# Layer norms of a graph network: mean and deviation applied by ScalarE instead of VectorE, biases and own features added by VectorE instead of TensorE

## The chip, the cores and the metric

The kernel runs on one core of a Trainium2 chip. The metric is the device time of one execution in microseconds (us). A core has five engines that run their own instruction streams and wait for each other by semaphores: TensorE (PE in the profile; PEld is its weight loading), VectorE (DVE), ScalarE (ACT), GpSimd (POOL) and SyncE (SP), which here issues transfers. Matmul results land in PSUM, everything else lives in SBUF with 128 partitions. A tile "128x512" has 512 elements in each of 128 partitions.

## The reference, cut to what matters

There are 16 graphs ("entries") of 1024 nodes with 64 features, each with a 1024 x 1024 weighted adjacency. Four layers follow each other; each adds its result to its input and applies a layer norm without learned scale:

```python
def _layernorm(x, axis=-1, eps=1e-5):
    m = jnp.mean(x, axis=axis, keepdims=True)
    v = jnp.var(x, axis=axis, keepdims=True)
    return (x - m) / jnp.sqrt(v + eps)

# layer 0: messages, then a two-layer MLP on [x, messages]
dh = jnp.tanh(jnp.concatenate([x, adj @ x], -1) @ W1 + b1) @ W2 + b2
x = _layernorm(x + dh)
# layer 1: mean over neighbours
x = _layernorm(x + (adj / jnp.clip(jnp.sum(adj, 2, keepdims=True), 1.0, None)) @ x)
# layers 2 and 3: thin out the neighbours, take per feature a weighted sum of the
# 0.25, 0.5 and 0.75 quantiles over each node's neighbours (agg), then an MLP
y = (relu((x + agg) @ W1 + b1) @ W2 + b2) * mask[..., None]
x = _layernorm(x + y)
```

So one entry has four layer norms, 64 in all.

## The kernel before

Nodes stand on partitions: one entry's features are a tile of 128 x (8 x 64), "NT = 8" tiles of 64 features, C = 64, processed in two halves of G = 4 tiles. For the quantiles, each node's neighbours are gathered by POOL from a table in memory into a ring (`got_s`), or, for the nodes with most neighbours, picked by matmuls with one-hot matrices (`hot`, `pgk`); VectorE sorts the gathered lists with min and max networks (`got_s`, `other`, `got`), and ScalarE multiplies the sorted rows by weights.

The order of the program is made by hand: the sorting of round k is the main thread, and the other parts (features and lists of later entries, the end of earlier ones) are Python generators. A counter adds up VectorE's estimated time, and `yield 7` means: the next piece of this generator is emitted once VectorE has been given about 7 us more of work. Each engine executes its own instructions in the emitted order.

The layer norm:

```python
def settle(dst, y, chain):
    st = s.work.tile([P, 4, NT], F32, name=f"ln_st_{chain}", bufs=1)
    dve.reduce_sum(st[:, 0], y, axis=AX.X)
    dve.tensor_scalar(st[:, 1], st[:, 0], 1.0 / C, None, op0=ALU.mult)
    dve.tensor_sub(y, y, st[:, 1, :, None].to_broadcast([P, NT, C]))
    yield 2
    nc.scalar.activation(dst, y, AF.Square)
    yield 7
    dve.reduce_sum(st[:, 2], dst, axis=AX.X)
    yield 1
    nc.scalar.activation(st[:, 3], st[:, 2], AF.Sqrt, bias=eps, scale=1.0 / C)
    yield 6
    dve.reciprocal(st[:, 0], st[:, 3])
    dve.tensor_mul(dst, y, st[:, 0, :, None].to_broadcast([P, NT, C]))
```

The first two layers, with cuts:

```python
def features(b, e):
    # ... x_s and the adjacency tiles adj[i] are loaded
    for h in range(NH):                     # two halves of 512 nodes
        # ... px: transposed x_s (L417) and messages (L421), node_in
        nc.tensor.matmul(px[:C], w01s, node_in, start=True, stop=True)
        yield 9
        nc.scalar.activation(hid_t, px[:C], AF.Tanh, bias=b01c)
        yield 3
        pd = s.psum.tile([P, G, C], F32, name="pd", tag="x", bufs=1)
        for q in range(G):
            nc.tensor.matmul(pd[:, q, :], hid_t[:, q * P : (q + 1) * P], w02s, start=True, stop=False)
            nc.tensor.matmul(pd[:, q, :], ones_row, bias_rows[0], start=False, stop=False)     # L438
            nc.tensor.matmul(pd[:, q, :], ident, x_s[:, h * G + q, :], start=False, stop=True) # L439
        yield 10
        nc.scalar.copy(y[:, h * G : (h + 1) * G], pd)                                          # L441
    yield 4
    yield from settle(x1[:, :, :C], y, "x")
    # ...
    for h in range(NH):
        # ... pa = adjacency times x1, with the row sum in column C (L454); near from adj
        dve.tensor_scalar(deg[:, 0], pa[:, :, C], 1.0, None, op0=ALU.max)
        dve.reciprocal(deg[:, 1], deg[:, 0])
        yield 1
        for q in range(G):                                                                     # L465
            nc.scalar.activation(y[:, h * G + q, :], pa[:, q, :C], AF.Copy, scale=deg[:, 1, q : q + 1])
    yield 5
    dve.tensor_add(y, y, x1[:, :, :C])
    yield from settle(x2, y, "x")
    # ...
```

The end of layers 2 and 3 (`agg` holds the quantile sums, `xc` the layer's input):

```python
def finish(b, e, layer, agg):
    for h in range(NH):
        pt = s.psum.tile([P, HALF], F32, name="pt", tag="m", bufs=1)
        for q in range(G):
            # transpose and add in PSUM: xc (L763), agg (L764)
            nc.tensor.matmul(pt[:C, q * P : (q + 1) * P], xc[:, h * G + q, :], ident, start=True, stop=False)
            nc.tensor.matmul(pt[:C, q * P : (q + 1) * P], agg[:, h * G + q, :], ident, start=False, stop=True)
        # ... o_t = copy of pt; ph = w1s times o_t; h_t = relu(ph + b1c)
        pd = s.psum.tile([P, G, C], F32, name="pd", tag="m", bufs=1)
        for q in range(G):
            nc.tensor.matmul(pd[:, q, :], h_t[:, q * P : (q + 1) * P], w2s, start=True, stop=False)
            nc.tensor.matmul(pd[:, q, :], ones_row, bias_rows[1 + layer], start=False, stop=True)  # L778
        yield 9
        for t in range(h * G, (h + 1) * G):                                                        # L781
            nc.scalar.activation(y[:, t, :], pd[:, t - h * G, :], AF.Copy, scale=e.mask[:, t : t + 1])
    yield 4
    dve.tensor_add(y, y, xc)
    yield from settle(xn, y, "m")
    # ... xn is written to the table of the next layer, or to the output, by eight POOL transfers
```

The one-hot selections, the largest user of PE, are emitted from `pick` (L349) for one row of 24 matmuls at a time, after VectorE has made the one-hot matrix `hot`, of which four can exist at once.

Of the kernel before, what the change touches and what calls it, by code (L numbers as in the profile page):

```python
# [12 lines left out]
F32 = mybir.dt.float32  # L13
# [4 lines left out]
AF = mybir.ActivationFunctionType  # L18
ALU = mybir.AluOpType
AX = mybir.AxisListType  # L20

P = 128
# [5 lines left out]
KS = -(-(max(SIZES[:-1]) - 1) // 8) * 8  # L28
KW = max(SIZES)
HOTS = 4  # L30
ROOM = 75
LONG = 40
BIG = 1e30
EPS = 1e-5
# [178 lines left out]
def adj_resnorm_kernel(ctx: ExitStack, tc: tile.TileContext, x, adj_t, nodemask, w01, b01, w02, b02,  # L213
                       w21, b21, w22, b22, w31, b31, w32, b32, out):
    nc = tc.nc
    B, N, C = x.shape
    NT = N // P
# [3 lines left out]
    s = SimpleNamespace()  # L221
    dve = Metered(nc.vector)
# [47 lines left out]
    def row(ap, name):  # L270
        return weight(ap.rearrange("(o c) -> o c", o=1), name)

    def column(ap, name):
        return weight(ap.rearrange("(c o) -> c o", o=1), name)

    w01s, b01c, w02s = weight(w01, "w01s"), column(b01, "b01c"), weight(w02, "w02s")
    mlps = [
        (weight(w21, "w21s"), column(b21, "b21c"), weight(w22, "w22s")),
        (weight(w31, "w31s"), column(b31, "b31c"), weight(w32, "w32s")),
    ]  # L280
    bias_rows = [row(b, f"bias_row{i}") for i, b in enumerate((b02, b22, b32))]
    ones_row = const.tile([1, P], F32, name="ones_row")
    nc.vector.memset(ones_row, 1.0)
# [78 lines left out]
    def settle(dst, y, chain):  # L362

        st = s.work.tile([P, 4, NT], F32, name=f"ln_st_{chain}", bufs=1)
        dve.reduce_sum(st[:, 0], y, axis=AX.X)
        dve.tensor_scalar(st[:, 1], st[:, 0], 1.0 / C, None, op0=ALU.mult)
        dve.tensor_sub(y, y, st[:, 1, :, None].to_broadcast([P, NT, C]))
        yield 2
        nc.scalar.activation(dst, y, AF.Square)
        yield 7  # L370
        dve.reduce_sum(st[:, 2], dst, axis=AX.X)
        yield 1
        nc.scalar.activation(st[:, 3], st[:, 2], AF.Sqrt, bias=eps, scale=1.0 / C)
# [17 lines left out]
    G = HALF // P  # L391

    def features(b, e):
# [18 lines left out]
        for h in range(NH):  # L412

            node_in = s.work.tile([P, HALF], F32, name="node_in", bufs=1)
            px = s.psum.tile([P, HALF], F32, name="px", tag="x", bufs=1)
            for q in range(G):
                nc.tensor.transpose(px[:C, q * P : (q + 1) * P], x_s[:, h * G + q, :], ident)  # L417
# [14 lines left out]
            hid_t = s.work.tile([C, HALF], F32, name="hid_t", tag="node_in", bufs=1)  # L432
            nc.scalar.activation(hid_t, px[:C], AF.Tanh, bias=b01c)
            yield 3
            pd = s.psum.tile([P, G, C], F32, name="pd", tag="x", bufs=1)
            for q in range(G):
                nc.tensor.matmul(pd[:, q, :], hid_t[:, q * P : (q + 1) * P], w02s, start=True, stop=False)
                nc.tensor.matmul(pd[:, q, :], ones_row, bias_rows[0], start=False, stop=False)  # L438
                nc.tensor.matmul(pd[:, q, :], ident, x_s[:, h * G + q, :], start=False, stop=True)  # L439
            yield 10  # L440
            nc.scalar.copy(y[:, h * G : (h + 1) * G], pd)  # L441
# [5 lines left out]
        for h in range(NH):  # L447
            pa = s.psum.tile([P, G, C + 1], F32, name="pa", tag="x", bufs=1)
            for q in range(G):
                i = NT + h * G + q  # L450
                t = i - NT
# [303 lines left out]
    def finish(b, e, layer, agg):  # L755

        xc = e.xs[layer]
        w1s, b1c, w2s = mlps[layer]
        y = s.work.tile([P, NT, C], F32, name="y_m", bufs=1)
        for h in range(NH):  # L760
            pt = s.psum.tile([P, HALF], F32, name="pt", tag="m", bufs=1)
            for q in range(G):
                nc.tensor.matmul(pt[:C, q * P : (q + 1) * P], xc[:, h * G + q, :], ident, start=True, stop=False)  # L763
                nc.tensor.matmul(pt[:C, q * P : (q + 1) * P], agg[:, h * G + q, :], ident, start=False, stop=True)  # L764
# [9 lines left out]
            yield 3  # L774
            pd = s.psum.tile([P, G, C], F32, name="pd", tag="m", bufs=1)
            for q in range(G):
                nc.tensor.matmul(pd[:, q, :], h_t[:, q * P : (q + 1) * P], w2s, start=True, stop=False)
                nc.tensor.matmul(pd[:, q, :], ones_row, bias_rows[1 + layer], start=False, stop=True)  # L778
            yield 9
            for t in range(h * G, (h + 1) * G):  # L780
                nc.scalar.activation(y[:, t, :], pd[:, t - h * G, :], AF.Copy, scale=e.mask[:, t : t + 1])  # L781
# [178 lines left out]
    def per_row(ap):  # L960
        t = s.work.tile([P, C], F32, name="per_row")
        nc.sync.dma_start(t, ap.rearrange("(o c) -> o c", o=1).to_broadcast([P, C]))
        return t

    def transposed(src, name):

        dst = s.work.tile([C, N], F32, name=name, bufs=1)
# [7 lines left out]
    def layer0(adj_half, x_s, x1):  # L975
# [21 lines left out]
        nc.vector.tensor_add(y, y, per_row(b02)[:, None, :].to_broadcast([P, NT, C]))  # L997
        nc.vector.memset(x1[:, :, C : C + 1], 1.0)
        layernorm(x1[:, :, :C], y)

# [15 lines left out]
        nc.vector.tensor_add(y, y, x1[:, :, :C])  # L1016
        layernorm(x2, y)

    def mlp(xc, agg, mask, layer, dst):
        w1s, b1c, w2s = mlps[layer]  # L1020
# [12 lines left out]
        nc.vector.tensor_add(y, pd, per_row((b22, b32)[layer])[:, None, :].to_broadcast([P, NT, C]))  # L1033
# [131 lines left out]
    with tc.If(nc.values_load(over_d[:, B:]) > 0):  # L1165
        with tc.For_i(0, B) as b:
            with tc.If(nc.values_load(over_d[:, ds(b, 1)]) > 0), ExitStack() as general:
# [32 lines left out]
                for layer, (xc, xn) in enumerate(((x2, x3), (x3, x1[:, :, :C]))):  # L1200
                    with tc.tile_pool(name=f"g_lists{layer}", bufs=1) as lists:
                        long_quantiles(lists, table[layer][0], idx, wts, agg)
                    with tc.tile_pool(name=f"g_dense{layer}", bufs=1) as dense:
                        dense_quantiles(dense, xc, valid, count, longest, agg)
                    mlp(xc, agg, mask, layer, xn)
# [34 lines left out]
```

## Time and profile before

| | |
|---|---|
| time, median of 3 runs | 5350.52 us (5345.66 to 5353.45) |
| span of the profiled execution | 5351.7 us, 110787 instructions |
| granted TensorE clock, mean | 0.745 of full speed |
| busiest groups on VectorE | min and max of the sorts; `hot` 449.3 us; near, takes, order |
| POOL | 2944 gathers, mean 1134 ns; 256 row writes |

The profile is of one execution. "Busy" is the time in which an engine executes; an engine that waits for a semaphore is not busy. A group line names line, engine and operation, output and inputs, the number of instructions, then busy us and mean ns of one, then the idle time just before them and what ended it. Line numbers of VectorE are mostly L207, a helper through which all its instructions of the main program pass; so VectorE's work is told apart by the tiles that it reads and writes. A line of waits reads: who waited, on whom, us in total, how many times, longest us. The chain that ended last consists of POOL's last output writes alone, so it does not show what set the time; the stages and the waits have to do it.

### The profile page before, as it was taken

How to read it: one execution, taken by the hardware profiler on the slowest of the kernel's cores; microseconds unless marked ns; L12 is line 12 of the kernel's file. 1: busy time of each engine (PE TensorE's matmuls, PEld its weight loads, DVE VectorE, ACT ScalarE, POOL GpSimd, SP SyncE). 2: the span in 40 equal slices, each digit the busy share in tenths (PEclk: the TensorE clock that was granted, in tenths of full speed). 3: DMA queues.
4: the chain of work that ended last, by engine and by line, in shares of the span. 5: the costliest groups of instructions: out<-in, count | busy, mean ns of one | idle time of the engine just before them, and what ended most of it. 6: DMA issues, size and time to landing. Idle time of an engine off the chain costs nothing. (4 is left out here: it accounts for less than half of the span.)

```text
span 5351.7 us, 110787 instructions
## 1 busy us (share of the span) xinstructions
PE 3747.4 (70%) x44869; PEld 2907.4 (54%) x44936; DVE 4588.7 (86%) x9200; ACT 2052.9 (38%) x5056; POOL 3650.5 (68%) x3228
## 2 busy tenths in 40 slices
PE   7857476778785866858588795949588695726343
PEld 5746255656574655647376573737476574625332
DVE  2495667999999989798998989999988999998976
ACT  2352342435352624435252624444343535212211
POOL 0425626777777777767677777787777878787572
PEclk7877677788686877868687787879687786756555
DMA  2212212222222221222222131222222221111010
GB/s 82 77 31 50 45 40 59 52 60 57 58 54 58 46 55 41 59 54 57 56 56 58 39 74 36 55 49 58 58 56 59 54 48 21 27 21 26 16 24 10
DMA packets 420176, 259.27 MB, mean 48 GB/s; under 512 B 106164, under 2 KB 368452, under 8 KB 419652
## 3 DMA queue, kind: packets, MB, share of 16 engines
q0 software_dynamic: 102400, 105.06, 10.2%
q1 hardware_dynamic: 317252, 147.02, 9.7%
q8 instruction: 353, 5.78, 0.5%
q14 instruction: 171, 1.40, 0.1%
HBM read 239.27 MB, written 12.58 MB: 47 GB/s over the span
## 5 line engine op out<-in xcount | busy, mean ns | idle before, releaser
L353 POOL DMA_INDIRECT got_s<-table,idx x2944 | 3338.6, 1134 | 1461.1 <-issue 775.9
L349 PEld LDWEIGHTS <-hot 128*128 128x128 bf16 x24576 | 977.3, 109 | 763.3 <-DVE hot L207 656.2
L349 PE MATMUL pgk<-x2p,hot 128*128 128x64 bf16 x12288 | 538.7, 210 | 340.1 <-DVE hot L207 331.9
L349 PE MATMUL pgk<-x3p,hot 128*128 128x64 bf16 x12288 | 543.3, 210 | 262.8 <-DVE hot L207 237.1
L512 PE MATMUL pr<-steps,near 128*128 128x512 bf16 x1469 | 403.1, 430 | 257.0 <-ACT junk L518 154.1
L207 DVE TENSOR_TENSOR other<-got_s 128x512 f32<-128x512 f32 (+8 forms) x900 | 516.4, 583 | 57.5 <-issue 35.9
L743 ACT ACTIVATE got_s<-got_s,wts 128x64 f32<-128x64 f32 x1568 | 400.8, 337 | 343.3 <-DVE got_s L207 342.6
L207 DVE TENSOR_SCALAR hot<-place 128x1024 bf16<-128x1024 f16 x1024 | 449.3, 441 | 89.0 <-PE pgk L349 88.7
L207 DVE TENSOR_TENSOR got_s<-got_s 128x384 f32<-128x384 f32 (+7 forms) x918 | 492.0, 538 | 19.0
L598 PE MATMUL pk<-near,order 128*128 128x512 f16 x2048 | 487.9, 394 | 17.3 <-DVE order L207 13.9
L454 PE MATMUL pa<-x,adj_r 128*128 128x65 f32 x2048 | 398.6, 379 | 134.8 <-DMA adj_r<-in_adj_dram 49.8
L454 PEld LDWEIGHTS pa<-x,adj_r 128*128 128x128 f32 x2048 | 387.1, 293 | 140.9 <-DMA adj_r<-in_adj_dram 50.1
L512 PEld LDWEIGHTS <-near 128*128 128x128 f16 x1536 | 162.0, 108 | 475.2 <-issue 349.6
L207 DVE TENSOR_TENSOR got_s<-other 128x512 f32<-128x512 f32 (+8 forms) x774 | 408.6, 540 | 7.2
L555 PE MATMUL pv<-minus_n,takes 128*128 128x128 bf16 x1024 | 206.3, 237 | 197.2 <-DVE takes L207 195.0
L598 PEld LDWEIGHTS <-order 128*128 128x128 bf16 x2048 | 200.0, 101 | 260.8 <-issue 41.0
L207 DVE TENSOR_TENSOR other<-other 128x128 f32<-128x128 f32 (+13 forms) x558 | 319.0, 572 | 14.9
L518 ACT ACTIVATE junk<-pr,nb_st 128x1024 f16<-128x1024 f32 x256 | 281.8, 1107 | 43.9 <-PE pr L512 42.8
L207 DVE TENSOR_TENSOR other<-got 128x128 f32<-128x128 f32 (+5 forms) x270 | 232.7, 881 | 59.1 <-ACT got L733 56.4
L421 PE MATMUL px<-adj_r,x_s 128*64 128x128 f32 x2048 | 272.3, 291 | 4.0 <-ACT node_in L424 2.9
L743 ACT ACTIVATE got<-got,wts 128x64 f32<-128x64 f32 x672 | 165.0, 335 | 268.0 <-DVE got L207 268.0
L421 PEld LDWEIGHTS px<-adj_r,x_s 128*64 128x64 f32 x2048 | 243.6, 147 | 22.5 <-issue 12.8
(201 smaller groups left out, 6953.6 us busy)
## 6 DMA issues: line engine op xcount, KB each, us to landing
adj_r<-in_adj_dram SPq DMA_DIRECT2D x256, 512.0 KB
got_s<-table,idx POOLq DMA_INDIRECT x2944
x_s<-in_x_dram SPq DMA_DIRECT2D x16, 256.0 KB
table<-x SPq DMA_DIRECT2D x16, 256.0 KB
x<-table SPq DMA_DIRECT2D x16, 256.0 KB
table<-x3s,rows POOLq DMA_INDIRECT x128
out_dram<-agg,out_rows POOLq DMA_INDIRECT x128
table<-no_row SPq DMA_DIRECT2D x6, 0.2 KB
```

The costliest lines, as they stand in the source:

```text
L207: return call(*args, **kwargs)
L349: nc.tensor.matmul(dst, hot[:, c, :], parts[:, c, q, :], start=first and c + q == 0, stop=c == NT - 1 and q == 2)
L353: nc.gpsimd.indirect_dma_start(out=dst, out_offset=None, in_=tab, in_offset=bass.IndirectOffsetOnAxis(ap=rows, axis=0))
L421: nc.tensor.matmul(px[C:, q * P : (q + 1) * P], x_s[:, jt, :], adj[t][:, jt, :], start=jt == 0, stop=jt == NT - 1)
L454: nc.tensor.matmul(pa[:, q, :], adj[i][:, jt, :], x1[:, jt, :], start=jt == 0, stop=jt == NT - 1)
L512: nc.tensor.matmul(pr[:, h * HALF : (h + 1) * HALF], near[:, c, t * P : (t + 1) * P], steps[:, ONSET + h * HALF - c * P :][:, :HALF], star ...
L518: nc.scalar.activation(junk, prs[t - 1], AF.Sign, bias=lim[:, i, t - 1 : t], scale=-1.0, accum_out=cut_at[:, i, t - 1 : t])
L555: nc.tensor.matmul(pv[:, cols], takes[:, c, rows], minus_n, start=False, stop=False)
L598: nc.tensor.matmul(cols, order[:, c, t * P : (t + 1) * P], left(c, slice(h * G, (h + 1) * G)), start=c == 0, stop=c == NT - 1)
L743: nc.scalar.activation(prods[:, m, i, :], got[:, m, slot_id, :], AF.Copy, scale=e.wts[:, t, i : i + 1])
```

## The change

In the layer norms ScalarE subtracts the mean and multiplies by the reciprocal deviation, one tile of 64 features at a time, because its per-partition bias and scale hold one value for each partition. VectorE loses these two passes. In exchange, what PE and ScalarE did for VectorE elsewhere goes back to it: the biases, the own features and the sum of `xc` and `agg` are no longer added by matmuls in PSUM, and the degree and the mask are no longer multiplied in by ScalarE. It is another division of the same work among the engines. The biases are now kept as rows spread over all partitions, and the space of the old bias rows lets the gather ring have one row more.

```diff
-ROOM = 75
+ROOM = 76
...
-    w01s, b01c, w02s = weight(w01, "w01s"), column(b01, "b01c"), weight(w02, "w02s")
+    w01s, b01c, w02s, b02r = weight(w01, "w01s"), column(b01, "b01c"), weight(w02, "w02s"), per_row(b02, "b02r")
... (b22r and b32r likewise, in place of bias_rows and ones_row)
@@ settle
-        dve.tensor_scalar(st[:, 1], st[:, 0], 1.0 / C, None, op0=ALU.mult)
-        dve.tensor_sub(y, y, st[:, 1, :, None].to_broadcast([P, NT, C]))
+        dve.tensor_scalar(st[:, 1], st[:, 0], -1.0 / C, None, op0=ALU.mult)
         yield 2
+        for t in range(NT):
+            nc.scalar.activation(y[:, t, :], y[:, t, :], AF.Identity, bias=st[:, 1, t : t + 1])
         nc.scalar.activation(dst, y, AF.Square)
-        yield 7
+        yield 9
         dve.reduce_sum(st[:, 2], dst, axis=AX.X)
         yield 1
         nc.scalar.activation(st[:, 3], st[:, 2], AF.Sqrt, bias=eps, scale=1.0 / C)
         yield 6
         dve.reciprocal(st[:, 0], st[:, 3])
-        dve.tensor_mul(dst, y, st[:, 0, :, None].to_broadcast([P, NT, C]))
+        yield 1
+        for t in range(NT):
+            nc.scalar.activation(dst[:, t, :], y[:, t, :], AF.Copy, scale=st[:, 0, t : t + 1])
+        yield 7
@@ features
-                nc.tensor.matmul(pd[:, q, :], hid_t[:, q * P : (q + 1) * P], w02s, start=True, stop=False)
-                nc.tensor.matmul(pd[:, q, :], ones_row, bias_rows[0], start=False, stop=False)
-                nc.tensor.matmul(pd[:, q, :], ident, x_s[:, h * G + q, :], start=False, stop=True)
+                nc.tensor.matmul(pd[:, q, :], hid_t[:, q * P : (q + 1) * P], w02s, start=True, stop=True)
             yield 10
-            nc.scalar.copy(y[:, h * G : (h + 1) * G], pd)
-        yield 4
+            dve.tensor_add(y[:, h * G : (h + 1) * G], pd, x_s[:, h * G : (h + 1) * G])
+        dve.tensor_add(y, y, b02r[:, None, :].to_broadcast([P, NT, C]))
...
-            yield 1
-            for q in range(G):
-                nc.scalar.activation(y[:, h * G + q, :], pa[:, q, :C], AF.Copy, scale=deg[:, 1, q : q + 1])
-        yield 5
+            dve.tensor_mul(y[:, h * G : (h + 1) * G], pa[:, :, :C], deg[:, 1, :, None].to_broadcast([P, G, C]))
@@ finish
+        dve.tensor_add(agg, agg, xc)
         for h in range(NH):
...
-                nc.tensor.matmul(pt[:C, q * P : (q + 1) * P], xc[:, h * G + q, :], ident, start=True, stop=False)
-                nc.tensor.matmul(pt[:C, q * P : (q + 1) * P], agg[:, h * G + q, :], ident, start=False, stop=True)
+                nc.tensor.transpose(pt[:C, q * P : (q + 1) * P], agg[:, h * G + q, :], ident)
...
-                nc.tensor.matmul(pd[:, q, :], h_t[:, q * P : (q + 1) * P], w2s, start=True, stop=False)
-                nc.tensor.matmul(pd[:, q, :], ones_row, bias_rows[1 + layer], start=False, stop=True)
+                nc.tensor.matmul(pd[:, q, :], h_t[:, q * P : (q + 1) * P], w2s, start=True, stop=True)
             yield 9
-            for t in range(h * G, (h + 1) * G):
-                nc.scalar.activation(y[:, t, :], pd[:, t - h * G, :], AF.Copy, scale=e.mask[:, t : t + 1])
-        yield 4
+            dve.tensor_add(y[:, h * G : (h + 1) * G], pd, b2r[:, None, :].to_broadcast([P, G, C]))
+        dve.tensor_mul(y, y, e.mask[:, :, None].to_broadcast([P, NT, C]))
         dve.tensor_add(y, y, xc)
```

The other lines of the change belong to a general path for graphs with more neighbours, which does not run on these inputs.

More of the change, by code (lines that the diff above doesn't have):

```diff
@@ L268, in weight, with per_row @@
         return t
-    def row(ap, name):
-        return weight(ap.rearrange("(o c) -> o c", o=1), name)
+    def per_row(ap, name):
+        t = const.tile([P, C], F32, name=name)
+        nc.sync.dma_start(t, ap.rearrange("(o c) -> o c", o=1).to_broadcast([P, C]))
+        return t
     def column(ap, name):
         return weight(ap.rearrange("(c o) -> c o", o=1), name)
-    w01s, b01c, w02s = weight(w01, "w01s"), column(b01, "b01c"), weight(w02, "w02s")
+    w01s, b01c, w02s, b02r = weight(w01, "w01s"), column(b01, "b01c"), weight(w02, "w02s"), per_row(b02, "b02r")
     mlps = [
-        (weight(w21, "w21s"), column(b21, "b21c"), weight(w22, "w22s")),
-        (weight(w31, "w31s"), column(b31, "b31c"), weight(w32, "w32s")),
-    ]
-    bias_rows = [row(b, f"bias_row{i}") for i, b in enumerate((b02, b22, b32))]
-    ones_row = const.tile([1, P], F32, name="ones_row")
-    nc.vector.memset(ones_row, 1.0)
+        (weight(w21, "w21s"), column(b21, "b21c"), weight(w22, "w22s"), per_row(b22, "b22r")),
+        (weight(w31, "w31s"), column(b31, "b31c"), weight(w32, "w32s"), per_row(b32, "b32r")),
+    ]
     mask_all = const.tile([P, B, NT], F32, name="mask_all")
@@ L757, in finish @@
         xc = e.xs[layer]
-        w1s, b1c, w2s = mlps[layer]
+        w1s, b1c, w2s, b2r = mlps[layer]
         y = s.work.tile([P, NT, C], F32, name="y_m", bufs=1)
+        dve.tensor_add(agg, agg, xc)
         for h in range(NH):
@@ L958, in layernorm @@
         nc.vector.tensor_mul(dst, y, st[:, 0, :, None].to_broadcast([P, NT, C]))
[L960 to L963, printed above, removed]
     def transposed(src, name):
@@ L996, in layer0 @@
         nc.vector.tensor_add(y, pd, x_s)
-        nc.vector.tensor_add(y, y, per_row(b02)[:, None, :].to_broadcast([P, NT, C]))
+        nc.vector.tensor_add(y, y, b02r[:, None, :].to_broadcast([P, NT, C]))
         nc.vector.memset(x1[:, :, C : C + 1], 1.0)
@@ L1017, in layer1, with mlp @@
         layernorm(x2, y)
-    def mlp(xc, agg, mask, layer, dst):
-        w1s, b1c, w2s = mlps[layer]
+    def mlp(xc, agg, mask, weights, dst):
+        w1s, b1c, w2s, b2r = weights
         y = s.work.tile([P, NT, C], F32, name="y")
@@ L1032, in mlp @@
             nc.tensor.matmul(pd[:, t, :], h_t[:, t * P : (t + 1) * P], w2s, start=True, stop=True)
-        nc.vector.tensor_add(y, pd, per_row((b22, b32)[layer])[:, None, :].to_broadcast([P, NT, C]))
+        nc.vector.tensor_add(y, pd, b2r[:, None, :].to_broadcast([P, NT, C]))
         nc.vector.tensor_mul(y, y, mask[:, :, None].to_broadcast([P, NT, C]))
@@ L1204, in adj_resnorm_kernel @@
                         dense_quantiles(dense, xc, valid, count, longest, agg)
-                    mlp(xc, agg, mask, layer, xn)
+                    mlp(xc, agg, mask, mlps[layer], xn)
                     if layer == 0:
```

## The prediction, made before the change was run

> **What bounds the kernel now.** I read the page's first two parts for the busiest engine and where in the span it is not busy, then the table by stage, then what VectorE (DVE) waits for in the middle of the run, then the groups of the operations that the change touches.
>
> ```profile
> PE 3747.4 (70%) x44869; PEld 2907.4 (54%) x44936; DVE 4588.7 (86%) x9200; ACT 2052.9 (38%) x5056; POOL 3650.5 (68%) x3228
> ...
> DVE  2495667999999989798998989999988999998976
> ```
>
> VectorE leads with 86%, and its row shows that the 14% of idle time is mostly at the two ends. The table by stage (columns: stretch, its length, then busy us and instructions of PE, PEld, DVE, ACT, POOL, then clock and DMA) puts numbers on that:
>
> ```profile
> 0.00:1000.00 1000.00, 694.22 (x7323) 532.98 (x7342) 614.35 (x1516) 365.16 (x755) 433.07 (x444) 0.75 0.22 55
> 1000.00:4500.00 3500.00, 2633.87 (x31871) 2030.55 (x31919) 3248.31 (x6128) 1492.75 (x3659) 2658.14 (x2296) 0.77 0.22 53
> 4500.00:5352.00 852.00, 419.31 (x5679) 343.92 (x5676) 726.06 (x1557) 194.96 (x644) 559.27 (x490) 0.61 0.10 21
> ```
>
> In the middle VectorE is busy 3248 of 3500 us, 93%. POOL looks free there (76%), but the timeline shows a pause of 0.30 us before nearly every gather: 2296 instructions x 0.30 = 689 us, so POOL is occupied for 2658 + 689 = 3347 us, 96%. Two engines are thus close to full, and neither PE (75%) nor ACT (43%) is. What VectorE waits for there:
>
> ```profile
> DVE hot L207 <- PE pgk L349: 57.6, 35, 5.1
> DVE other L207 <- ACT got L733: 46.0, 8, 14.4
> DVE y_m L207 <- ACT y_m L781: 15.7, 4, 9.0
> DVE deg L207 <- PE pa L454: 15.1, 6, 3.7
> ```
>
> These four are 134 us, and the whole list about 160 us. The first two say that PE is late with the one-hot selections (L349). PE takes its work in order, so a burst of something else in front makes it late.
>
> **What the Trainium skill says, and whether this trace agrees.** "ScalarE: Activation LUTs", section "What ACT_TABLE_LOAD costs": an ACTIVATE with a per-partition pointer operand takes about 280 ns + 0.833 ns per element, and two back to back overlap by some 93 ns. For 64 elements that gives an estimate of 333 ns, or 240 ns in a row. The trace has it: 337 ns for the 128x64 products (L743), and 21 of them in 5.12 us at the end, 244 ns each. The same page, "Table sets: the hidden batching unit", says that cheap functions such as identity and copy are in every set. No Identity runs in this kernel; but its Copy, Sign and Abs run between Sqrt and Tanh, and there are only 24 + 23 + 1 table loads. So I expect none more. "VectorE: DVE Perf Modes", section "The perf-mode tier table", puts an fp32 tensor_tensor at the same 1x from SBUF and from PSUM. The trace agrees: 128x512 with one input in PSUM (place from pp) takes 684 ns, like 684 to 692 from SBUF.
>
> **The change, VectorE first.** Per entry (there are 16) four layer norms lose two 128x512 operations of 692 ns: 8 x 0.692 = 5.54 us less. What comes back: in the features two 128x256 additions from PSUM, one 128x512 bias addition and two 128x256 multiplications by the degree; with 425 ns for 128x256 (the sort's rows give 421 to 428) that is 4 x 0.425 + 0.685 = 2.39 us. Each of the two MLP ends gets one 128x512 addition (0.684), two 128x256 additions (0.85) and one 128x512 mask product (0.69): 2.23 us, twice 4.45. Sum 6.84 us. The change therefore **adds** 6.84 - 5.54 = 1.30 us per entry to VectorE, 16 x 1.30 = **21 us** in all. On a full engine that is on the path. VectorE should read about 4610 us.
>
> **ScalarE.** 64 operations of 128x64 are added per entry, 1024 in all. L743 takes 400.8/1568 = 0.256 us of busy time each, so +262 us. Gone are the degree scales (L465, 29.7 us), the mask scales (L781, 58.7) and the copies of pd (L441, 12.0): -100 us. ACT rises to about 2215 us, still under half, and most of it lies beside VectorE's work. A layer norm gets longer by latency, though: eight operations in a row are 1.95 us in place of 0.86 us of VectorE with its hand-over, twice per norm, about 2.5 us. Where the schedule has other work for VectorE that is hidden; the code adds 9 to 10 units of distance per norm for it.
>
> **PE.**
>
> ```profile
> L778 PE MATMUL pd<-bias_row,ones_row 1*128 1x64 f32 x512 | 132.9, 346 | 0.0
> L764 PE MATMUL pt<-ident,agg 128*64 128x128 f32 x512 | 116.0, 314 | 28.8 <-DVE agg L207 28.8
> L439 PE MATMUL pd<-x_s,ident 128*128 128x64 f32 x256 | 70.2, 366 | 0.0
> L438 PE MATMUL pd<-bias_row,ones_row 1*128 1x64 f32 x256 | 67.9, 353 | 0.0
> L417 PE MATMUL px<-ident,x_s 128*64 128x128 f32 x128 | 24.6, 326 | 15.3 <-ACT y_x L441 11.8 <-DMA x_s<-in_x_dram 3.5
> ```
>
> Bias and own-feature matmuls go: 132.9 + 67.9 + 70.2 = 271 us. L764 and its pair L763 (59.1 + 61.8) together take 237 us, because an fp32 matmul leaves two records per instruction (512 for 256). A real transpose leaves one: L417 has 128 for 16 x 8, at 24.6/128 = 0.19 us of busy time. 256 of those are 49 us, saving another 188. PE falls by 459 us, 28.7 per entry, to about 3290 us. Bursts in front of the selections shrink: pd of an MLP half from 5 to 2.5 us, its transposes from about 5 to 1.3.
>
> How much of that reaches the end? PE is not full, so only VectorE's waits count. In the timeline the longest wait for hot (5.8 us, at 4919 us) follows directly on a pd burst of 5 us, and the one of 1.4 us at 2198 us on another; but those at 2220 and 2528 us follow the order matmuls (L598), which stay. I take a sixth of the 134 us plus what the ends hold: **-20 us**. Against it stand new waits: VectorE itself now reads pd, for which only ACT waited before, at 64 + 32 places where 64 + 32 halves end. The distance after the matmuls is 9 to 10 units instead of 13 to 14 up to VectorE's next reader, while the burst is 2.5 to 4 us shorter, so each place is about as safe as y_m now is, but there are twice as many. y_m costs 15.7 us in the middle; I add **+15 us** for the first halves and the features.
>
> **The ends.** At the start nothing hides the chain. In the first layer the pd burst of each half takes 6.2 us (30.72 to 36.9) for 12 pairs of records; eight of the twelve go, about -3.9 us each half. The layer norm's +2.5 and the bias addition's +0.7 come back, so -4.4 us; the second layer has no PE saving and a second norm with +2.5. I book -4 us. At the end I walked the chain from the last aggregation (5312.9 us): +0.7 for the addition that now stands first, transposes that can no longer run ahead (+1.3), then -2.5 for each pd, -1.5 for the second transposes, -0.5 for each copy of pd, +0.7, and +2.5 for the norm; it comes out level, and the eight writes can start with the first normalised tile instead of the last, about 1.5 us earlier. Ends together: **-6 us**.
>
> The room of the gather ring goes from 75 to 76 rows. Laying the tiles out by the code's rule (sizes 19, 17, 15, 14, 13, 11, 10, wrapping when the next does not fit) gives the same places for both, so I book nothing.
>
> **Sum**: 5350.5 + 21 - 20 + 15 - 6 = 5360.5, and I predict **5360 us**.
>
> **Rivals.** (1) *PE relief wins.* If most of the 134 us were set by the removed bursts, some 60 us would go: 5350 + 21 - 60 - 6 = about 5305. For it: waits right behind pd bursts, and a PE clock of 0.77 that may rise with less fp32 work. Against: most of L598, L454 and L421, which are larger, stays. (2) *ScalarE's new blocks stand in the way.* ACT also runs in order; a block of eight that waits for VectorE's statistics holds up the copies of pgk, codes and products behind it. If each of the 64 norms cost VectorE 1 us more, +64: about 5425. For it: VectorE already waits 46 us for ACT's copy of pgk. Against: 57% of ACT is idle in the middle. (3) *POOL sets the round.* It is occupied 96%, its instructions do not change, and then 21 us more on VectorE vanish in its slack: about 5340 to 5350. Against: POOL waits 85.5 us for VectorE's sort in the middle and VectorE hardly for gathers (2.7 us). (4) *The order shifts.* The program's order is made by counting VectorE's estimated time, so every changed operation moves others; that can go either way by 20 to 30 us.
>
> **Range and chances.** The first two rivals are the edges of what I think likely, and both need most of the waits to go one way. Range 5320 to 5405 us. 2% is 107 us, below 5243 or above 5458, which none of the rivals reaches: chances 0.02 faster, 0.94 within 2%, 0.04 slower; slower gets more because VectorE's load goes up for certain.
>
> **What would show it.** Right: VectorE about 4610 us, PE about 3290, ACT about 2215, table loads still 48, and waits of VectorE on PE's pd of 10 to 30 us. If waits for hot and got fall by more than 50 us, rival 1 holds; if waits of VectorE on ACT rise by more than 40 us, rival 2. The prediction is wrong at its base if VectorE's busy time does not rise, if Identity brings table loads (64 x 1.28 us), or if the first or last 500 us change by over 20 us.

## The result, and the profile after

| | before | after |
|---|---|---|
| time, median of 4 runs each | 5351.05 us (5345.66 to 5353.45) | 5320.66 us (5318.06 to 5321.83) |
| after / before | | 0.9944, 95% interval 0.9927 to 0.9961 |
| span of the profiled execution | 5351.7 us | 5320.1 us |
| granted TensorE clock, mean | 0.745 | 0.736 |

The change makes the kernel 30 us faster, 0.56%. It gives VectorE, the engine that bounds it, more to do, and takes work from PE, which is busy for less of the time. The first view is the page's busy times and VectorE's row of slices, to be held against the first fence of the prediction:

```profile
PE 3372.3 (63%) x43084; PEld 2586.5 (49%) x43144; DVE 4606.9 (87%) x9279; ACT 2208.3 (42%) x5662; POOL 3671.4 (69%) x3228
...
DVE  2685758999988989899998999999898989998976
```

VectorE has 18 us more (4588.7 before), PE 375 us less, ACT 155 us more. The table by stage (stretch, length, then busy us and instructions of PE, PEld, DVE, ACT, POOL, then clock and DMA):

```profile
0.00:1000.00 1000.00, 632.39 (x7194) 486.21 (x7213) 639.93 (x1568) 400.81 (x893) 451.52 (x461) 0.77 0.23 58
1000.00:4500.00 3500.00, 2397.73 (x30741) 1825.44 (x30782) 3258.93 (x6190) 1597.47 (x4076) 2687.48 (x2298) 0.76 0.23 53
4500.00:5321.00 821.00, 342.15 (x5153) 274.83 (x5150) 708.03 (x1523) 210.04 (x694) 532.39 (x471) 0.60 0.10 21
```

In the first 1000 us VectorE now gets 1568 instructions done in place of 1516: it is further on in the program when the middle begins. In the middle PE has 236 us less to do. What VectorE waits for there, in the kernel after (who waits, for whom, us in total, times, longest us):

```profile
DVE hot L207 <- PE pgk L348: 58.4, 29, 6.9
DVE other L207 <- ACT got L731: 52.7, 11, 10.2
DVE deg L207 <- PE pa L455: 14.6, 5, 3.3
DVE y_m L207 <- PE pd L775: 12.5, 6, 2.5
```

The first two were 57.6 and 46.0. With 236 us less of PE work the waits for PE's selections are no shorter.

To see where the gain came from, the sort can serve as a clock. VectorE executes 18 rounds of sorting, each of 306 min and max instructions, in both kernels. The start of a round, taken from the trace as that of its first such instruction, shows how far each kernel has come:

| us | before | after | after - before |
|---|---|---|---|
| round 0 | 254.5 | 234.7 | -19.8 |
| round 1 | 507.2 | 473.7 | -33.5 |
| round 2 | 823.8 | 784.2 | -39.6 |
| round 4 | 1420.2 | 1397.4 | -22.8 |
| round 5 | 1716.4 | 1721.8 | +5.4 |
| round 8 | 2664.5 | 2632.7 | -31.8 |
| round 10 | 3273.3 | 3231.1 | -42.2 |
| round 14 | 4473.6 | 4446.4 | -27.2 |
| end | 5351.7 | 5320.1 | -31.6 |

When round 2 starts the kernel after is 39.6 us ahead, more than the whole gain. The lead doesn't stay as it is: at round 5 it is gone, at round 10 it is 42.2 us. In round 4 alone, which is 28 us longer after, VectorE waits 20.8 us for `hot` and 10.2 for `got`, before 2.1 and 4.9. On balance rounds 2 to 13 lose 12.4 us (3649.8 us before, 3662.2 after), and the last four rounds with the end bring back 4.4. So the table shows where the lead arises; that it lasts to the end because of the start takes an experiment (e6 below).

### The profile page after: what moved, and what is told of

Read it like the earlier page. It is cut to its first block, busy times and chain, and to the rows that moved or that the text cites. A ratio compares the mean times of both kernels' runs of the same rounds, so it can differ in the third digit from the quotient of the medians.

```text
span 5320.1 us, 107953 instructions
## 1 busy us (share of the span) xinstructions
PE 3372.3 (63%) x43084; PEld 2586.5 (49%) x43144; DVE 4606.9 (87%) x9279; ACT 2208.3 (42%) x5662; POOL 3671.4 (69%) x3228
## 4 chain that ended last, share of the span: by engine, by line
DVE 69%; PE 14%; POOL 5%; issue 5%; ACT 3%; DMA 3%; DVEq 0%; POOLq 0%; SPq 0%; ACTq 0%
DVE other L207 22%; DVE got_s L207 17%; DVE got L207 10%; DVE hot L207 5%; POOL got_s L352 4%; DVE best L207 4%; PE pgk L348 3%; PE pk L596 3%; PE pa L455 3%; DMA got_s<-table,idx 2%; DVE less L207 2%; PE px L424 1%; PE ordered_x L348 1%; DVE y_m L207 1%; DVE y_x L207 1%
## 5 line engine op out<-in xcount | busy, mean ns | idle before, releaser
L348 PEld LDWEIGHTS <-hot 128*128 128x128 bf16 x24576 | 997.8, 110 | 682.5 <-DVE hot L207 568.2
L348 PE MATMUL pgk<-x2p,hot 128*128 128x64 bf16 x12288 | 550.1, 211 | 213.4 <-DVE hot L207 202.5
L510 PE MATMUL pr<-steps,near 128*128 128x512 bf16 x1476 | 433.0, 452 | 313.0 <-ACT junk L516 190.0
L207 DVE TENSOR_TENSOR other<-got_s 128x512 f32<-128x512 f32 (+8 forms) x900 | 516.0, 584 | 49.2 <-issue 28.8
L596 PE MATMUL pk<-near,order 128*128 128x512 f16 x2048 | 473.7, 385 | 20.6 <-ACT code L607 13.9
L455 PE MATMUL pa<-x,adj_r 128*128 128x65 f32 x2048 | 383.3, 369 | 153.1 <-DMA adj_r<-in_adj_dram 92.2
L455 PEld LDWEIGHTS pa<-x,adj_r 128*128 128x128 f32 x2048 | 372.5, 284 | 155.8 <-issue 134.7
L762 PE MATMUL pt<-ident,agg 128*64 128x128 f32 x256 | 52.8, 344 | 488.1 <-DVE agg L207 462.9
L424 PE MATMUL px<-adj_r,x_s 128*64 128x128 f32 x2048 | 270.4, 290 | 13.4 <-DMA adj_r<-in_adj_dram 11.4
L762 PEld LDWEIGHTS pt<-ident,agg 128*64 128x64 f32 x256 | 29.5, 135 | 500.6 <-DVE agg L207 459.6
```

The lines of the kernel that those rows point to most:

```text
L207: return call(*args, **kwargs)
L348: nc.tensor.matmul(dst, hot[:, c, :], parts[:, c, q, :], start=first and c + q == 0, stop=c == NT - 1 and q == 2)
L455: nc.tensor.matmul(pa[:, q, :], adj[i][:, jt, :], x1[:, jt, :], start=jt == 0, stop=jt == NT - 1)
L510: nc.tensor.matmul(pr[:, h * HALF : (h + 1) * HALF], near[:, c, t * P : (t + 1) * P], steps[:, ONSET + h * HALF - c * P :][:, :HALF], star ...
L596: nc.tensor.matmul(cols, order[:, c, t * P : (t + 1) * P], left(c, slice(h * G, (h + 1) * G)), start=c == 0, stop=c == NT - 1)
L762: nc.tensor.transpose(pt[:C, q * P : (q + 1) * P], agg[:, h * G + q, :], ident)
```

## The experiments

**Theory A** says that the gain is the shorter bursts on PE at the start. There no sorting hides anything: VectorE can't sort before the first lists are made, the lists need PE, and PE takes what the features of entries 1 to 3 and the first MLP ends have put in front of them. **Theory B** says that the norms on ScalarE bring the start forward (VectorE has less between features and lists). **Theory C** says that the changed order of the program does it, since the counter that spaces the generators sees other costs.

On three of the four chips that ran these experiments PE's instructions arrived late, and the kernel before took 7594 to 7709 us there. So each ratio is one against the kernel before on the same chip, and only the runs on the fourth chip (e5, e6), with 5347 us before, stand in the same conditions as the result.

### The halves of the change: e1, e5 (norms only), e2, e9 (additions only)

e1 and e5 are the same kernel: the kernel before with the new `settle`, distances included, and nothing else.

```diff
 def settle(dst, y, chain):
-    dve.tensor_sub(y, y, mean); yield 2; Square; yield 7; ...; dve.tensor_mul(dst, y, reciprocal)
+    yield 2; 8 x Identity(bias = -mean); Square; yield 9; ...; yield 1; 8 x Copy(scale = reciprocal); yield 7
```

> The kernel before with only the layer norm changed (mean and deviation by ScalarE; biases, own features, degree and mask stay with PE and ScalarE). Theory A (the gain of the whole change is PE's removed bursts at the start, where PE stands in the chain): the start does not get shorter, the third round of sorting still begins at about 820 to 830 us (before: 823.8, after: 784.2); later VectorE is 89 us less busy (about 4500 us), of which part reaches the end because POOL is 96% occupied: 5280 to 5330 us. Rival B (the gain comes from the norms' move): the third round begins at about 785 to 800 us already here.

Measured: 7217.62 us against 7709.31, ratio 0.9366 (0.9346 to 0.9386); the third round (round 2) starts at 1094.8 us.

> The same kernel as the first run with the norms alone, again, because there every matmul instruction reached PE late and the kernel before took 7709 us. Where the kernel before takes about 5350 us: Theory A: the third round of sorting begins at 815 to 830 us (before 823.8), VectorE's busy time is about 4504 us as in the first run, and the time is 5280 to 5330 us. Rival B (the gain of the change comes from the norms' move): the third round begins at 785 to 800 us.

Measured: 5447.97 us (5446.65 to 5450.44) against 5347.09, ratio 1.0188 (1.0171 to 1.0205); the third round starts at 870.7 us. Both expectations missed. The same kernel is 6% faster on one chip and 2% slower on the other. What it does at a normal supply of PE's instructions shows in the busy times of e5's page:

```profile
PE 3821.1 (70%) x44839; PEld 2985.8 (55%) x44936; DVE 4499.4 (83%) x9072; ACT 2301.0 (42%) x6084; POOL 3649.9 (67%) x3228
```

and in VectorE's waits in e5 from 1000 to 4500 us:

```profile
DVE hot L207 <- PE pgk L349: 163.9, 47, 9.2
DVE other L207 <- ACT got L737: 74.3, 9, 12.0
DVE y_m L207 <- ACT y_m L785: 24.1, 5, 10.0
```

VectorE is relieved of 89 us (4499.4 in place of 4588.7), and the kernel is 100 us longer. The wait for the selections in the middle goes from 57.6 to 163.9 us and the one for ACT's copy of `got` from 46.0 to 74.3. So half of the change, taken alone, is a loss although it lightens the fullest engine. Theory B falls: with the norms alone the third round starts 47 us later than before (823.8), not earlier. Nearly all of these 47 us are lost in round 0 (298.2 us long, 252.6 before) and won back by round 8; the 100 us are lost from round 9 on. Why was not tested.

e2 and e9 are the same kernel too: the kernel after with the old `settle`, so PE's relief and the added work of VectorE without the gain in the norms.

```diff
 # the kernel after, but in settle:
-    8 x Identity ...; 8 x Copy ...
+    dve.tensor_sub(...); ...; dve.tensor_mul(...)      # and the distances 2, 7, 1, 6 of before
```

> The changed kernel with the old layer norm on VectorE (biases, own features, sums, degree and mask on VectorE). Theory A: the third round begins at about 785 us as in the changed kernel; VectorE is about 89 us busier than after (4696 us), and most of that is paid in the middle: 5370 to 5410 us. Rival B: the third round begins at about 820 us, and the time is above 5420 us.

Measured: 7615.63 against 7709.31 us, ratio 0.9883 (0.9866 to 0.99); third round 1038.0 us.

> The same kernel as the first run with additions alone (old layer norm on VectorE), again. Where the kernel before takes about 5350 us: Theory A: third round at 780 to 795 us; VectorE is about 107 us busier than before (4696 us), and the time is 5370 to 5420 us. Rival B (the gain comes from the norms' move): third round at about 820 us, above 5420 us.

Measured: 7492.72 against 7594.29 us, 0.9855 (0.9809 to 0.9901); third round 1015.9 us. With PE's instructions late, this half is faster even though VectorE has 4691.4 us of work (e2). Where the kernel before takes 5350 us it was not run.

### Why the late chips can't settle it: what bounds there

The profile of e10 (the kernel after with a few matmuls more, below) on such a chip has these busy times:

```profile
PE 4036.9 (53%) x43368; PEld 2876.9 (38%) x43368; DVE 4609.0 (61%) x9279; ACT 2210.6 (29%) x5662; POOL 3312.8 (44%) x3228
```

The longest of PE's waits in e10 over the whole run:

```profile
PE pgk L348 <- issue: 1134.0, 1305, 3.3
```

"issue" means that PE waited for nothing the profile shows: its next instruction was not there. That is 1134 us in the selections alone; in all lines together the trace has 2118 such gaps with 2025 us, and in the kernel after at 5320 us 25 gaps with 22 us. PE's busy time and these gaps together are 80% of the 7596 us, while VectorE is busy for only 61%. So there PE with its late instructions is the fuller of the two, on the fourth chip VectorE is, and a change that moves work between them can have another value on each.

### The bursts at the start: e3, e6; later: e4, e10

Both take the kernel after and give PE back about what the change took from it, but for a few entries only: dummy matmuls into the same PSUM tile, overwritten by the real ones. In e3 and e6 that is in the features of entries 0 to 3 and the first MLP ends of entries 0 and 1; in e4 and e10 in those of entries 8 to 11 and of 8 and 9. e6 repeats e3 and e10 repeats e4. At the MLP ends it is somewhat more, since the transpose stays beside the two matmuls: the four blocks of transposes of entries 0 and 1 take 11.0 us before, 3.3 after and 16.5 in e6. Nothing is counted by the counter, so all other instructions stand in the order of the kernel after.

```diff
+if b in (0, 1, 2, 3):                                  # e4, e10: (8, 9, 10, 11)
+    nc.tensor.matmul(pd[:, q, :], ident[:1, :], w02s[:1, :], start=True, stop=True)
+    nc.tensor.matmul(pd[:, q, :], ident, x_s[:, h * G + q, :], start=True, stop=True)
 nc.tensor.matmul(pd[:, q, :], hid_t[...], w02s, start=True, stop=True)
 ...
+if layer == 0 and b in (0, 1):                         # e4, e10: (8, 9)
+    # two matmuls of xc with ident ahead of each transpose, one of bias size ahead of each pd matmul
```

> The changed kernel, with matmuls of the removed sizes put back in front of the real ones, their results overwritten, only for the features of entries 0 to 3 and the first MLP ends of entries 0 and 1; program order and all other engines' work unchanged. Theory A: the third round begins 25 to 40 us later than after (810 to 825 us) and the time is 5340 to 5360 us. Rival C (the gain is the new order of the program): third round within 5 us of after, 5315 to 5326 us.

Measured: 7741.36 against 7709.31 us, ratio 1.0041 (1.0025 to 1.0056); third round 1072.5 us.

> The same number of put-back matmuls as in the run with bursts at the start, but for entries 8 to 11 (features) and 8 and 9 (MLP ends), in the middle of the run. Theory A: PE has room there, so the time rises by 0 to 8 us over after: 5320 to 5329 us. If PE's bursts cost as much in the middle as at the start, 5340 us or more.

Measured: 7719.28 against 7709.31 us, 1.0012 (1.0 to 1.0024); third round 1019.7 us, 52.8 us earlier than in e3. On this chip the later bursts cost as well: e4 loses about 30 of its 50 us of lead over e3 between rounds 8 and 13.

> The same kernel as the first run with put-back matmuls in entries 8 to 11, again. Where the kernel before takes about 5350 us: Theory A: third round as after (784), time 5318 to 5329 us, since in the middle PE has room. If such bursts cost as much there as at the start (37 us): 5350 us or more.

Measured: 7586.74 against 7594.29 us, 0.9982 (0.9966 to 0.9997). Two chips, and both within half a per cent of the kernel before. On neither is VectorE the fuller engine, so whether the same bursts cost as much in the middle of a run of 5350 us as at its start stays open.

> The same kernel as the first run with put-back matmuls at the start, again. Where the kernel before takes about 5350 us: Theory A: the third round begins at 810 to 825 us (after 784.2) and the time is 5340 to 5360 us. Rival C (the new order of the program): third round within 5 us of 784, 5315 to 5326 us.

Measured: 5357.8 us (5353.83 to 5363.81) against 5347.09, ratio 1.0022 (1.0012 to 1.0031) where the kernel after has 0.9944. The third round starts at 832.3 us, a little above what was expected, and the time is inside. At round 2 e6 is 48.1 us behind the kernel after (before: 39.6), at the end 37, and more than the whole gain is gone. From round 4 to round 14 its distance to the kernel after stays between 37.5 and 38.1 us: nothing is caught up, nothing is added. So e6 has the swings of the middle too (43.1 us behind the kernel before at round 5, 4.6 ahead at round 10), and nearly the same waits there (57.9 us for `hot`, 52.3 for `got`). They belong to what e6 shares with the kernel after, the order and the other division of work, and not to the bursts of the start; which of the two makes them was not tested.

How it happens is seen in PE's timeline around the first lists (start us, duration us, line, output and inputs; in brackets the idle time before and what ended it). Before:

```profile
162.46 0.68 PE L437 MATMUL pd<-w02s,hid_t 64*128 64x64 f32 x2 [3.29 <-ACT hid_t L433]
163.07 0.68 PE L438 MATMUL pd<-bias_row,ones_row 1*128 1x64 f32 x2
163.68 0.69 PE L439 MATMUL pd<-x_s,ident 128*128 128x64 f32 x2
...
169.22 0.69 PE L439 MATMUL pd<-x_s,ident 128*128 128x64 f32 x2
170.38 1.06 PE L417 MATMUL px<-ident,x_s 128*64 128x128 f32 x4 [0.46 <-ACT y_x L441]
171.37 5.90 PE L421 MATMUL px<-adj_r,x_s 128*64 128x128 f32 x32
177.20 3.63 PE L598 MATMUL pk<-near,order 128*128 128x512 f16 x16
```

After, the same place:

```profile
152.05 1.97 PE L440 MATMUL pd<-w02s,hid_t 64*128 64x64 f32 x8 [3.29 <-ACT hid_t L436]
154.54 1.06 PE L420 MATMUL px<-ident,x_s 128*64 128x128 f32 x4 [0.52 <-DVE y_x L207]
155.53 4.92 PE L424 MATMUL px<-adj_r,x_s 128*64 128x128 f32 x32
160.43 4.89 PE L596 MATMUL pk<-near,order 128*128 128x512 f16 x16
```

And in e6:

```profile
163.50 0.69 PE L441 MATMUL pd<-w02s,ident 1*128 1x64 f32 x2 [3.29 <-ACT hid_t L436]
...
170.27 0.69 PE L443 MATMUL pd<-w02s,hid_t 64*128 64x64 f32 x2
171.48 1.06 PE L420 MATMUL px<-ident,x_s 128*64 128x128 f32 x4 [0.52 <-DVE y_x L207]
172.47 5.06 PE L424 MATMUL px<-adj_r,x_s 128*64 128x128 f32 x32
177.47 3.63 PE L599 MATMUL pk<-near,order 128*128 128x512 f16 x16
```

Read each from the first `pd` to the first `pk`, which are the order matmuls of the first lists. Of the 16.8 us by which `pk` starts earlier after the change (177.20 to 160.43), 10.4 are there already when this burst begins, from the bursts ahead of it, and 6.4 come in it: 7.4 us from the first `pd` to its end before (162.46 to 169.91), 2.0 after. In e6 it is 7.5 us again, and `pk` stands at 177.47, 0.3 us from where it was before the change.

The burst is dear there because PE runs at half its clock. In the kernel before the same 12 pairs take 7.45 us here and 4.42 us at 1058.2 us, where the granted clock is 1.00. The kernel before in stretches of 5 us (columns as in the table by stage; the clock is the third number from the right):

```profile
165.00:170.00 5.00, 4.91 (x16) 3.90 (x16) 0.00 (x0) 5.00 (x11) 0.00 (x0) 0.50 0.00 0
170.00:175.00 5.00, 4.62 (x21) 4.17 (x22) 3.43 (x9) 0.32 (x2) 0.00 (x0) 0.50 0.00 0
175.00:180.00 5.00, 5.00 (x30) 3.31 (x29) 0.00 (x0) 0.58 (x1) 0.00 (x0) 0.91 0.64 185
180.00:185.00 5.00, 5.00 (x88) 4.08 (x87) 0.39 (x4) 1.20 (x2) 0.00 (x0) 1.00 0.10 29
```

The Trainium skill, "TensorE: Matmul & The Clock Gate", section "What's actually happening", says that PE runs at half rate by default and after an idle window of about 3.4 us, and at full rate after some 3.4 us of sustained work. The trace has both rates, 0.50 in the burst and 1.00 later, but the way back is longer: the burst starts at 162.46 us, PE is busy nearly all the time from then on, and the full clock comes only between 175 and 180 us, after some 13 us. In the kernel after it comes some 6 us after the burst's start. Here the trace decides. From 160 to 170 us, while the burst runs, DVE is busy for 0 us: there is nothing that this burst lies beside.

The lists of entries 0, 1 and 2 follow it: ACT's copy of the sorted own keys starts at 182.5, 428.7 and 745.2 us before, at 166.9, 402.1 and 712.2 after, and at 182.7, 427.7 and 747.4 in e6. Theory A is shown, as far as "enough to explain": these bursts alone, put back in an unchanged order, restore the old starts and take the gain. Theory C falls for the start, since e6 has the order of the kernel after, and Theory B once more, since e6 has the norms on ScalarE. That the rest of the change comes out nearly level is a balance of swings and not shown to be more. One difference remains: in e6 VectorE itself waits for the longer `pd`, as the waits from 100 to 850 us show, where before ACT did; so its 37 us are lost in part on another path than the 30 were gained.

```profile
DVE y_m L207 <- PE pd L783: 48.5, 4, 22.7
DVE y_x L207 <- PE pd L443: 35.7, 6, 14.0
```

In the kernel after, the same two waits in the same stretch:

```profile
DVE y_m L207 <- PE pd L775: 24.2, 2, 12.2
...
DVE y_x L207 <- PE pd L440: 10.1, 3, 8.0
```

### Order against work: e7, e11 (norms in the old order), e8, e12 (the change in the old order)

e7 and e11 do the norms on ScalarE as e1 does, but the counter is charged for the removed passes and the distances are the old ones, so the order stays that of the kernel before. e8 and e12 do the same for the whole change: VectorE's added instructions are not counted, the old distances stand.

```diff
 # e7, e11: kernel before; e8, e12: kernel after
+    dve.us += 0.13 + NT * C / 960      # in place of each removed VectorE pass
     8 x Identity / 8 x Copy            # yields 2, 7, 1, 6, none after the Copy block
 # e8, e12 also
-    dve.tensor_add(y..., pd, ...)      # counted
+    nc.vector.tensor_add(y..., pd, ...)   # not counted; yields 10, 4; 1, 5; 9, 4 as before
```

> The norms alone on ScalarE, as in the run that took 5448 us, but the counter that makes the program's order is still charged for VectorE's two removed passes and the old distances are kept, so that everything is emitted in the order of the kernel before. Order theory (the 98 us came from the shifted order, which lets the selections meet lists, features and MLP ends on PE in each round): 5290 to 5350 us, rounds 9 to 13 of about 300 us in place of 317. Rival (ScalarE's blocks of eight hold up what stands behind them): 5420 to 5460 us, as with the shifted order.

Measured: 7588.62 against 7594.29 us, ratio 1.0007 (0.9986 to 1.0029).

> The norms alone on ScalarE in the order of the kernel before, again, as the first run of it had PE's instructions arriving late. Where the kernel before takes about 5350 us: order theory: 5290 to 5350 us, and each round from 9 to 13 about 300 us or less (317 with the shifted order). Rival (ScalarE's blocks of eight hold up what stands behind them): 5420 to 5460 us.

Measured: 7714.12 against 7703.49 us, 1.0018 (1.0001 to 1.0034).

> The whole change, but the counter is charged as in the kernel before (removed passes counted, added ones not, old distances), so the order is that of the kernel before. Theory A (PE's shorter bursts at the start give about 40 us, VectorE's 21 us more are paid later): third round at 780 to 795 us, time 5315 to 5345 us. If the new order gave the gain: 5350 us or more.

Measured: 7436.32 against 7594.29 us, 0.9783 (0.9739 to 0.9826).

> The whole change in the order of the kernel before, again. Where the kernel before takes about 5350 us: Theory A: third round at 780 to 795 us (before 823.8, after 784.2), time 5315 to 5345 us. If the new order gave the gain: third round above 815 us and 5350 us or more.

Measured: 7538.46 against 7703.49 us, 0.9793 (0.9767 to 0.9819).

All four ran on chips with late PE instructions, so they answer only part of the question. There the norms on ScalarE, 89 us less for VectorE, are worth nothing in the old order (1.0007, 1.0018) and 6% in the new one (0.9366). The same work in two orders differs by more than the whole change brings in any of these runs. The whole change in the old order gains 2.1 to 2.2% in each of the two; in the new one, with the few later bursts of e4 and e10, it is level (1.0012, 0.9982). In one and the same order, that of the kernel before, the whole change starts its third round 33.5 us (e8 against e7: 1013.0, 1046.4) and 38.7 us (e12 against e11: 1020.3, 1059.0) earlier than the norms alone, about as much as the 39.6 us of the result: on these chips too the start doesn't need the new order. **Left open**: whether on a chip with PE's normal supply it is the order or the blocks of eight on ScalarE that costs e5 its 100 us, and whether the change in the old order would be faster than 5320 us. Neither was run at 5350 us.

## Why the prediction was right in range and wrong in sign

The forecast was 5360 us in 5320 to 5405 and 0.94 for within 2%. The time is inside the lower edge by 0.7 us, less than the runs differ among each other (5318.06 to 5321.83), so that it is inside is luck. The prediction said 10 us slower; it is 30 us faster.

**Its VectorE step held.** 21 us of additional work were predicted and 4610 us in all; it is 4606.9. In rounds 2 to 13 VectorE's busy time grows by 10.2 us (3373.5 to 3383.7) and its idle time by 2.2 (276.3 to 278.5), which is the 12.4 us of the middle. The forecast for the middle, +21 - 20 + 15 = +16, is near it, but in part by luck: the 12.4 us are the balance of 45 us lost up to round 5 and 48 won back up to round 10, which no term foresaw, and the terms themselves were not all right:

- **The failed step in the middle is "-20 us" from PE's relief.** The waits for `hot` and `got` were to fall, and they went from 57.6 + 46.0 to 58.4 + 52.7. That the longest wait for hot follows on a `pd` burst did not make the burst its cause in general. A possible reason stands in the groups of the kernel after:

```profile
L762 PE MATMUL pt<-ident,agg 128*64 128x128 f32 x256 | 52.8, 344 | 488.1 <-DVE agg L207 462.9 <-DVE y_m L207 25.1
```

PE now stands 463 us at the head of the MLP ends, waiting for VectorE's addition of `xc`, where before it stood 28.8 us and could take `xc` ahead of it. In the middle this is 214 us, close to the 236 us of relief. PE's freed time became waiting in front of the same queue. Whether that alone kept the waits for hot where they are was not tested.
- **"+15 us" of new waits** was right in kind and near in size: y_m waits 12.5 us for PE's `pd` in the middle; the wait of 15.7 us for ACT's y_m that it replaces is gone, and y_x waits for `pd` only at the start (43.6 us of the run). Over the whole run VectorE's waits for `pd` are 50.8 + 43.6 = 94.4 us, far above the 10 to 30 that were to show the prediction right; the excess lies at the two ends.

**The mis-sized term is "The ends", -6 us: its -4 for the start measured -39.6.** That step walked the two halves of entry 0 and found -3.9 us for each burst, then took the norms' latency off again (its own terms add up to about -2, not -4). The burst itself was sized a little small: for the first one it is 5.1 us (6.19 to 1.10), for the one in the timeline above 5.5. What it missed is how many there are: before VectorE sorts round 2, the features of four entries and the first MLP ends run through PE's queue ahead of some list that VectorE waits for. The eight `pd` bursts of these features, each from its first to its last matmul, take 50.0 us together before and 11.4 after. It took the chain of one entry for the chain of the start. The prediction had also named the sign of its own failure, "if the first or last 500 us change by over 20 us"; the first 500 changed by 33 us (round 1).

**The end held.** From the last aggregation addition to the first output write it is 22.0 us, 24.3 before: -2.3 for -1.5 predicted. The timeline of the end, after:

```profile
5301.10 2.02 ACT L368 ACTIVATE y_m<-y_m,ln_st_m 128x64 f32<-128x64 f32 x8 [4.90 <-DVE ln_st_m L207]
...
5305.11 2.02 ACT L378 ACTIVATE agg<-y_m,ln_st_m 128x64 f32<-128x64 f32 x8 [0.27 <-DVE ln_st_m L207]
5305.73 0.97 POOL L785 DMA_INDIRECT out_dram<-agg,out_rows  x1 [71.42 <-ACT agg L378]
```

A block of eight takes 2.02 us (1.95 predicted), and the first write starts 0.6 us into the block, not after it.

**PE's busy time** fell by 375 us, not 459. The groups that went were read as sums of single matmuls, but L763 and L764 follow each other in turn, and in the timeline before (412.64 to 414.35 us) merged records 0.63 us long start every 0.43 us. They overlap, so the groups' busy times can't be added. Taken together, PE's matmuls into `pt` are busy for 158.0 us before (the prediction added up 237) and 52.8 after, 105 us less where 188 were expected: that is nearly all of the error. Those into `pd` fell by 283 us (413.1 to 129.9), where 271 were expected.

**ScalarE and the tables** held: 2208.3 us for 2215 predicted. Identity brought no loads of its own: 23 + 22 + 1, before 24 + 23 + 1:

```profile
L368 ACT ACTIVATE y_x<-y_x,ln_st_x 128x64 f32<-128x64 f32 x256 | 64.6, 335 | 315.0 <-DVE ln_st_x L207 315.0
...
L373 ACT ACT_TABLE_LOAD x23 | 29.5, 1283 | 0.4
L436 ACT ACT_TABLE_LOAD x22 | 28.2, 1283 | 0.4
```

This is what the Trainium skill says in "ScalarE: Activation LUTs", "Table sets: the hidden batching unit", and 335 ns is what its pointer operand's estimate gave (333).

**The rivals.** (1), PE's relief, was right about the sign and wrong about the place: not the waits of the middle, but the start. (2), ScalarE's blocks in the way, did not come true for the whole change (the wait for got rose by 6.7 us), and e5 leaves it possible for the half. (3), POOL's slack, did not hide VectorE's work in the middle: 10.2 us more busy time there, 12.4 us more time. (4), the order, was given 20 to 30 us; the pair e1 and e7 shows that it can be 6% where PE's instructions are late, and the swings of 45 and 48 us in the middle, whose cause is not shown, exceed it on the other chip too.

## What to carry to other kernels

The start has its own bound: where nothing is there yet to hide work, count every burst that stands ahead of the first result in an in-order engine's queue, of all the items being prepared and not only of the first, at the clock that PE has there. Two kernels whose bounding engine does the same instructions in the same rounds are compared by the start of each round, and of every round, since a few rounds picked out can hide swings as large as the gain. Freeing an engine that is not full is worth what its consumers wait for, and half of a change can lose more than the whole gains, so halves are measured before they are added up.

## What the runs showed of the hardware

- On three of the four chips PE's instructions came late: in e10 2025 us in 2118 gaps, most of them in the selections with their 24576 matmuls, for a kernel of 5350 us that took 7594 to 7709 us. The cause wasn't looked for. Two chips can turn the verdict on a kernel round: e1 and e5 are one kernel, 0.9366 and 1.0188.
- VectorE pays nothing for reading PSUM here: its 128x256 operations with `pd` or `pa` as an input take 417 to 425 ns in the median, and those from SBUF in the sort 418 to 425.
